# A graph kernel whose GpSimd gathers and scatters also wait for TensorE's place in the timetable, with a group's first gathers spread out

## The chip, the core and the metric

One core of a Trainium2 chip. The metric is device time in microseconds of one execution. The kernel before takes 2197.76 us, the median of three runs (2191.9 to 2199.88).

## What is computed

Two graph layers over 16 batches of 1024 nodes with 256 features, all in fp32. The first is an attention, the second weighs the edges of the adjacency matrix `adj` by a score of their two ends:

```
feats  = x @ W1.T;  f = feats @ w2 + b2
h      = softmax(leaky_relu(f[:,None] + f[None,:]) + adj) @ feats + bias2 + x
hidden = relu((h @ Wu)[u] + (h @ Wv)[v] + b1)             # for each pair u, v
S      = sigmoid(hidden @ w2' + b2')
z      = beta1*h + beta2*(((S*adj).T @ h) @ Wa + ba) + beta3*(((adj.T @ h) * h) @ Wm + bm)
```

`adj` is sparse, and S is needed only where it is not zero.

## The kernel before

The kernel computes S on the edges alone. At the start it makes a list of them: 135 slots of 128 edges, the same for all batches. The batches go in four groups of four, since one row that is gathered for an edge carries four batches.

For each batch TensorE does the attention: transposes (`turn`, `turn_e`), features, logits, products with the exponentials (`attend`, line 991, tile `pv`), then the ends of the edges (`end`, line 1028, tile `pp`), whose rows go to DRAM as `pu_d` and `pw_d`. VectorE takes `pv` out of PSUM in `keep_h` (lines 1002 and 1005, tiles `inv` and `xh`), and ScalarE copies the transposed result in `keep_hT` (line 1022, tile `hT`). The messages (line 1090, tile `pm`) and their products (line 1110, tile `pz`, taken up at line 1120) belong to the last term.

When the four batches of a group have their ends in DRAM, the group's 135 slots are scored (`scores`, line 1205), beside the attention of the next group. For a slot k:

- `fetch` (line 1140): GpSimd gathers, by an indirect DMA, 128 rows of `pw_d` into a `gv` buffer (line 1151, 1088 floats a row), and for the first slot of each of 21 lists also 128 rows of `pu_d` into `gu` (line 1144). There are 8 `gv` buffers, and slot k + 6 is fetched at the time of slot k (`AHEAD` is 6).
- `compare` (line 1180): VectorE, two instructions a slot, max and min of the two rows, in place.
- `sums` (lines 1191 and 1194): the sum over a row, on VectorE for some slots and on ScalarE for the others. This ends the use of the `gv` buffer.
- `gates`, and an addition (line 1221): the sigmoid of some 16 slots together, in a tile `lg`.
- `scatter` (line 1160): GpSimd writes 128 times four scores into `sa_d` in DRAM. Scatters that are ready wait in the list `late` and are emitted one or two a slot.

The scores of the first three groups fall into the time of the attention. After it, TensorE multiplies the scored edges by `h @ Wa` (`gather`, line 1284, tile `pzg`), which needs `sa_d` back in SBUF (`sat`, loaded by SP), turned by ScalarE (`part_sa`, line 1267) and multiplied by `adj` on VectorE (`weigh_sa`, line 1272). The fourth group is scored beside this work for the other groups, and its own product stands last.

The order of each engine's instructions comes from a timetable written by hand. `times.at(time, emit)` enters a piece of work at a moment; `times.matmuls(columns, emit)` enters TensorE's work at `times.now`, and moves that on by four cycles a column at 2.4 GHz. At the end all entries run in the order of their times, and each engine executes its instructions in that order, waiting only for data and free buffers. The times themselves play no part on the chip.

```
def at(self, time, emit):
    self.entries.append((time, len(self.entries), emit))

def matmuls(self, columns, emit):
    self.at(self.now, emit)
    self.now += columns * 4 / 2400
```

A group's slots share its stretch from `start` to `end` equally. In the function `first` of slot k stand the fetch of slot k + 6 and then the scatters of that moment; that of slot 0 is put 15 us earlier, and fetches slots 0 to 5 as well.

Of the kernel before, what the change touches and what calls it, by code (L numbers as in the profile page):

```python
# [14 lines left out]
P = 128  # L15
# [13 lines left out]
SLOTS = [(t, s) for t, width in enumerate(WIDTHS) for s in range(width)]  # L29
# [341 lines left out]
def edge_layers(  # L371
# [36 lines left out]
    nc = tc.nc  # L408
    B, N, D = x.shape
    C = N // P  # L410
    H = D // P
# [6 lines left out]
    p2 = ctx.enter_context(tc.tile_pool(name="p2", bufs=2, space=PSUM))  # L418
    ctx.enter_context(tc.manual_schedule())


    ident = const.tile([P, P], F32, name="ident")
    make_identity(nc, ident)
# [77 lines left out]
    for i in range(H):  # L501
        pt = p1.tile([P, BANK], F32, tag="p1", name="pt")
        for o in range(H):
            nc.tensor.transpose(pt[:, o * P : (o + 1) * P], w1_in[:, o, i * P : (i + 1) * P], ident)
        nc.vector.tensor_copy(w1T[:, i, :D], pt[:, :D])
        pw = p1.tile([P, BANK], F32, tag="p1", name="pw")
        for o in range(H):
            nc.tensor.matmul(
                pw[:, :1],
                lhsT=w1_in[:, o, i * P : (i + 1) * P],  # L510
                rhs=w2_col0[:, o, :],
                start=(o == 0),
                stop=(o == H - 1),
            )
        nc.vector.tensor_scalar(w1T[:, i, D : D + 1], pw[:, :1], 1.0 - SLOPE, None, ALU.mult)
# [36 lines left out]
    def rank_columns():  # L552
        nc.vector.tensor_scalar(up, w2_k, 0.0, None, ALU.is_ge)
        ps = p1.tile([P, BANK], F32, tag="p1", name="ps")
        nc.tensor.matmul(ps[:, 0:H], lhsT=upper, rhs=up, start=True, stop=True)
        nc.tensor.matmul(ps[:, H : 2 * H], lhsT=ones, rhs=up, start=True, stop=True)
        nc.vector.tensor_copy(signs, ps[:, : 2 * H])

    def place_columns():
# [31 lines left out]
    def turn_columns(i):  # L591
        pt = turned_w["pt", i] = p2.tile([P, 2 * BANK], F32, tag="p2", name="pt2")
        for k in range(H):
            for h in range(H):
                nc.tensor.transpose(
                    pt[:, (k * H + h) * P : (k * H + h + 1) * P],
                    uv_in[:, i, h, k * P : (k + 1) * P],
                    ident,
                )
# [7 lines left out]
    def sort_columns(i, h):  # L607
        pw = p1.tile([P, BANK], F32, tag="p1", name="pw")
        for k in range(H):
            nc.tensor.matmul(  # L610
                pw[:, :R],
                lhsT=turned_w[i][:, k, h * P : (h + 1) * P],
                rhs=to_place[:, i, k, :],
                start=(k == 0),
                stop=(k == H - 1),
            )
        nc.scalar.copy(wuv[:, i, h, :], pw[:, :R])

    def sort_bias():
        pw = p1.tile([P, BANK], F32, tag="p1", name="pw")  # L620
        for k in range(H):
            nc.tensor.matmul(
                pw[:, :R],
                lhsT=b1_rep[:, k, :],
                rhs=to_place[:, 0, k, :],
                start=(k == 0),
                stop=(k == H - 1),
            )
        nc.vector.tensor_copy(bu, pw[:, :R])
        nc.vector.memset(bu[:, HALF - 1 : HALF], -BIG)  # L630
# [22 lines left out]
    def edges():  # L653
# [76 lines left out]
        def placed():  # L730
# [20 lines left out]
            flat = pieces.rearrange("p k l -> p (k l)")  # L751
            yield
            pc = p1.tile([P, BANK], F32, tag="p1", name="pc")
            nc.tensor.matmul(pc[:, 0:K], lhsT=upper, rhs=flat, start=True, stop=True)
            nc.tensor.matmul(pc[:, K : 2 * K], lhsT=ones, rhs=flat, start=True, stop=True)
            yield
            total = keep.tile([P, K], F32, name="total0")
            nc.vector.tensor_copy(total, pc[:, K : 2 * K])
# [41 lines left out]
            nc.vector.tensor_reduce(over[:, 0:1], worst, AX.X, ALU.max)  # L800
            yield
            pl = p1.tile([P, BANK], F32, tag="p1", name="pl")
            nc.tensor.matmul(pl[:, :1], lhsT=ones, rhs=over[:, 0:1], start=True, stop=True)
            nc.vector.tensor_scalar(bad, pl[:, :1], 0.0, None, ALU.is_gt)
            yield

# [80 lines left out]
    def turn(b, h):  # L887

        pt = st["turn", b, h] = p2.tile([P, 2 * BANK], F32, tag="p2", name="pt2")
        for q in range(C):  # L890
            nc.tensor.transpose(
                pt[:, q * P : (q + 1) * P], held[b][:, q, h * P : (h + 1) * P], ident
            )

# [12 lines left out]
    def rows_of_f(b):  # L907

        pr = st["pr"] = p2.tile([P, 2 * BANK], F32, tag="p2", name="pr")
        for c in range(C):  # L910
            nc.tensor.transpose(
                pr[:, c * P : (c + 1) * P],
                st["f99"][:, c : c + 1].to_broadcast([P, P]),
                ident,
            )
# [5 lines left out]
    def features(b, c2):  # L921
        pf = st["pf", c2] = p2.tile([P, 2, BANK], F32, tag="p2", name="pf")
        for i in range(2):
            c = 2 * c2 + i
            for h in range(H):
                nc.tensor.matmul(  # L926
                    pf[:, i, : D + 1],
                    lhsT=st["xT"][:, h, c * P : (c + 1) * P],
                    rhs=w1T[:, h, :],
                    start=(h == 0),  # L930
                    stop=(h == H - 1),
                )
# [44 lines left out]
    def turn_e(b, c):  # L977
        e = st.pop(("e", b, c))
        pt = st["pt", b, c] = p2.tile([P, 2 * BANK], F32, tag="p2", name="pt2")
        for j in range(C):  # L980
            nc.tensor.transpose(pt[:, j * P : (j + 1) * P], e[:, j * P : (j + 1) * P], ident)  # L981

    def keep_eT(b, c):
        eT = st["eT", b, c] = two.tile([P, C, P], F32, name="eT")
# [2 lines left out]
    def attend(b, c):  # L987
        eT = st.pop(("eT", b, c))
        pv = st["pv", b, c] = p1.tile([P, BANK], F32, tag="p1", name="pv")
        for j in range(C):  # L990
            nc.tensor.matmul(  # L991
                pv[:, : D + 1],
                lhsT=eT[:, j, :],
                rhs=st["feats", b][:, j, :],
                start=(j == 0),
                stop=(j == C - 1),
            )
# [9 lines left out]
    def turn_h(b, i):  # L1007
        ph = st["ph", b, i] = p1.tile([P, H, 2 * P], F32, tag="p1", name="ph")
        for h in range(H):
            for k in range(2):  # L1010
                nc.tensor.transpose(
                    ph[:, h, k * P : (k + 1) * P],
                    held[b][:, 2 * i + k, h * P : (h + 1) * P],
                    ident,
                )
# [8 lines left out]
    def end(b, i, side, k):  # L1024

        pp = st["pp", side, k] = p1.tile([P, BANK], F32, tag="p1", name=f"pp{side}")
        for h in range(H):
            nc.tensor.matmul(  # L1028
                pp[:, :R],
                lhsT=st["hTi", b, i][:, h, k * P : (k + 1) * P],  # L1030
                rhs=wuv[:, side, h, :],
                start=(h == 0),
                stop=(h == H - 1),
            )
# [19 lines left out]
    def weighed(b, i):  # L1054
        pp = st["pea"] = p1.tile([P, 2, D], F32, tag="p1", name="pea")
        for k in range(2):
            for h in range(H):
                nc.tensor.matmul(  # L1058
                    pp[:, k, :],
                    lhsT=st["hTi", b, i][:, h, k * P : (k + 1) * P],  # L1060
                    rhs=wa[:, h, :],
                    start=(h == 0),
                    stop=(h == H - 1),
                )
# [21 lines left out]
    def message(b, half, h):  # L1086
        span = slice(half * BANK, (half + 1) * BANK)
        pm = st["pm", h] = p1.tile([P, BANK], F32, tag="p1", name="pm")
        for c in range(C):
            nc.tensor.matmul(  # L1090
                pm,
                lhsT=held[b][:, c, h * P : (h + 1) * P],
                rhs=adj_sb[:, c, span],
# [11 lines left out]
    def product(b, i):  # L1105
        pz = st["pz", i] = p1.tile([P, 2, D], F32, tag="p1", name="pz")
        for k in range(2):
            at = (2 * i + k) * P % BANK
            for h in range(H):
                nc.tensor.matmul(  # L1110
                    pz[:, k, :],
                    lhsT=st["mT"][:, h, at : at + P],
                    rhs=wm[:, h, :],
# [21 lines left out]
    AHEAD = 6  # L1135
# [4 lines left out]
    def fetch(g, k):  # L1140
        t, s = SLOTS[k]
        if s == 0:
# [5 lines left out]
                in_offset=bass.IndirectOffsetOnAxis(ap=key_u[:, t : t + 1], axis=0),  # L1148
            )
        gv = st["gv", k] = pools["gath"].tile([P, G * R], F32, name="gv", bufs=GV)  # L1150
        nc.gpsimd.indirect_dma_start(  # L1151
            out=gv,
            out_offset=None,
            in_=pw_d[g],
            in_offset=bass.IndirectOffsetOnAxis(ap=idx_v[:, t, s : s + 1], axis=0),
        )

    def scatter(g, lg, i, k):
        t, s = SLOTS[k]
# [7 lines left out]
        )  # L1167
        tc.declare_no_dep(dma.ins, group=f"sa{g}", reason="edges of their own")
        tc.add_to_no_dep_group(f"sa{g}", dma.ins)

    def by_batch(tile):
        return tile.rearrange("p (g r) -> p g r", r=R)
# [32 lines left out]
    def scores(g, start, end, on_vector):  # L1205

        for k in range(len(SLOTS)):
            time = start + k * (end - start) / len(SLOTS)

            def first(k=k):  # L1210
                for n in range(AHEAD) if k == 0 else ():
                    fetch(g, n)
                if k + AHEAD < len(SLOTS):
                    fetch(g, k + AHEAD)
                for _ in range(min(len(late), 2 if len(late) > PARTS[0] - 4 else 1)):
                    late.pop(0)()

            def last(k=k):
# [4 lines left out]
                )  # L1223
                late.extend(lambda i=i: scatter(g, lg, i, k0 + i) for i in range(k1 - k0))

            times.at(time - (15.0 if k == 0 else 0.0), first)
            times.at(time + 0.1, lambda k=k: compare(k, 0))
            times.at(time + 0.9, lambda k=k: compare(k, 1))
            k0, k1 = place_of(k)
# [46 lines left out]
    def gather(g, vc, part):  # L1276
# [4 lines left out]
        if part == C // 2 - 1:  # L1281
            order.sort(key=lambda cj: cj[1])
        for c, j in order:
            nc.tensor.matmul(  # L1284
                st["pzg", g, vc][:, j, :],
                lhsT=apart[:, c, j, :],
                rhs=st["ha", g, 2 * part + c][:, j * D : (j + 1) * D],
# [223 lines left out]
    def check():  # L1511
# [3 lines left out]
        nc.vector.tensor_reduce(ends_f[:, 1:2], f_least, AX.X, ALU.min)  # L1515
        pe = p1.tile([P, BANK], F32, tag="p1", name="pe")
        for i in range(2):
            nc.tensor.matmul(
                pe[0:1, i * P : (i + 1) * P],
                lhsT=ends_f[:, i : i + 1],  # L1520
                rhs=ident,
# [164 lines left out]
```

## Time and profile before

| | |
|---|---|
| Median of three runs | 2197.76 us (2191.9 to 2199.88) |
| Span of the profiled execution | 2373.8 us |
| TensorE matmul busy | 2185.9 us (92%) |
| VectorE, ScalarE busy | 1729.1, 1450.4 us |
| GpSimd busy | 1393.5 us, of it gathers of `gv` 599.7 and scatters 626.6 |
| Mean granted TensorE clock | 0.962 |
| DMA: gathers and scatters' queue, SP's queue | 46.4%, 31.3% of 16 engines' span |

The profile is of one execution that was recorded as it ran; its own time is the span, from the first instruction to the last, and nothing of the execution lies around it in the record. A row of a group of instructions reads: line, engine, operation, tile written and tiles read, shapes, how many; busy time and mean of one in ns; then how long the engine stood idle just before them, and what ended most of that. "issue" means that the engine waited for nothing that the profile shows, and "remote" or "another core or an unknown queue" that the record doesn't name the releaser. "POOL" is GpSimd, "DVE" VectorE, "ACT" ScalarE, "PEld" the loads of TensorE's weights.

### The profile page before, as it was taken

To read this page: it belongs to the slowest core of one execution; us is meant where nothing else is said; L and a number is where in the kernel's file an instruction comes from. 1 tells how busy PE (TensorE), PEld (TensorE's weight loads), DVE (VectorE), ACT (ScalarE), POOL (GpSimd) and SP (SyncE) were. 2 spreads that over 40 slices of the span, in tenths; PEclk is the share of its full clock that TensorE was granted. 3 is DMA by queue.
4 is the path that set the end of the run, shared out by engine and by line. 5 is a ranking of instruction groups with operands and counts; after the bars stand their busy time and mean duration, and the time that the engine had idled before them with its cause. 6 is when DMAs were issued, how large, how long until landed. Compare 5 with 4: busy or idle time off the path is not lost.

```text
span 2373.8 us, 30418 instructions
## 1 busy us (share of the span) xinstructions
PE 2185.9 (92%) x9478; PEld 1678.3 (71%) x9478; DVE 1729.1 (73%) x2660; ACT 1450.4 (61%) x3820; POOL 1393.5 (59%) x1277
## 2 busy tenths in 40 slices
PE   7999999798888989999899888988889999999998
PEld 6888877576666676766676666667557768778687
DVE  6599658687676777777777776777658879889454
ACT  5544567475656565657575555657347778778454
POOL 2223125677667767666777666667657767777400
PEclk9999999899899999999999998989999999999999
DMA  6789888677777777777787777778799999999664
GB/s 237 261 322 337 303 328 255 200 248 226 231 229 228 235 237 240 225 218 237 232 247 240 232 224 218 228 219 274 253 327 369 355 367 404 357 407 404 232 221 148
DMA packets 282491, 638.19 MB, mean 269 GB/s; under 512 B 43218, under 2 KB 142546, under 8 KB 281042
## 3 DMA queue, kind: packets, MB, share of 16 engines
q0 software_dynamic: 109312, 349.81, 46.4%
q1 hardware_dynamic: 154450, 268.93, 31.3%
q10 hardware_dynamic: 18560, 17.44, 2.2%
q8 instruction: 77, 1.26, 0.2%
q14 instruction: 92, 0.75, 0.1%
HBM read 476.42 MB, written 159.78 MB: 268 GB/s over the span
## 4 chain that ended last, share of the span: by engine, by line
PE 62%; DVE 16%; issue 6%; ACT 6%; another core or an unknown queue 5%; DMA 2%; POOL 1%; SPq 0%; POOLq 0%; ACTq 0%; DVEq 0%
PE pzg L1284 19%; PE pm L1090 12%; PE pv L991 11%; DVE gv L1180 7%; PE pp L1028 7%; PE pf L926 4%; PE pz L1110 3%; PE pea L1058 3%; DVE lg L1191 3%; PE pt L981 2%; ACT gv L1194 2%; DVE e L969 2%; ACT e L962 1%; DMA xh<-in_x_dram 1%
## 5 line engine op out<-in xcount | busy, mean ns | idle before, releaser
L1151 POOL DMA_INDIRECT gv<-pw_d,idx_v x540 | 599.7, 1111 | 382.3 <-ACT gv L1194 161.1
L1194 ACT ACTIVATE gv<-gv 128x272 f32<-128x272 f32 x1380 | 575.8, 420 | 362.8 <-DVE gv L1180 241.4
L1180 DVE TENSOR_TENSOR gv<-gv,gu 128x544 f32<-128x544 f32 x1080 | 735.2, 719 | 0.0
L1160 POOL DMA_INDIRECT sa_d<-lg,idx_s x540 | 626.6, 1160 | 181.2 <-issue 154.2
L991 PE MATMUL pv<-feats,eT 128*128 128x257 f32 x2048 | 480.7, 386 | 29.9 <-issue 21.1
L1090 PE MATMUL pm<-adj_sb,xh 128*128 128x512 f32 x1024 | 456.3, 598 | 7.5 <-issue 6.4
L1284 PE MATMUL pzg<-ha_g,apart 128*128 128x256 f32 x2048 | 450.4, 381 | 12.5 <-issue 12.5
L991 PEld LDWEIGHTS pv<-feats,eT 128*128 128x128 f32 x2048 | 385.7, 192 | 96.8 <-issue 33.9
L1284 PEld LDWEIGHTS pzg<-ha_g,apart 128*128 128x128 f32 x2048 | 391.2, 191 | 75.3 <-issue 22.0
L1090 PEld LDWEIGHTS pm<-adj_sb,xh 128*128 128x128 f32 x1024 | 194.5, 192 | 236.2 <-issue 232.4
L1028 PE MATMUL pp<-wuv,hT 128*128 128x272 f32 x1024 | 280.0, 420 | 67.4 <-ACT hT L1022 35.5
L1267 ACT COPY apart<-sat 128x1024 f32<-128x1024 f32 x128 | 255.5, 2005 | 70.0 <-PE pzg L1284 52.7
L1028 PEld LDWEIGHTS pp<-wuv,hT 128*128 128x128 f32 x1024 | 201.3, 203 | 124.4 <-ACT hT L1022 41.7
L1194 ACT ACTIVATION_READ_ACCUMULATOR gv<-gv 128x1 f32 x1380 | 261.2, 189 | 0.0
L1191 DVE TENSOR_REDUCE lg<-gv 128x4 f32<-128x1088 f32 x195 | 250.5, 1284 | 5.3
L1272 DVE TENSOR_TENSOR apart<-apart,adj_sb 128x1024 f32<-128x1024 f32 x128 | 156.7, 1224 | 99.2 <-ACT apart L1267 79.0
L969 DVE CUSTOM_DVE_ANT_0 e<-e,adj_sb 128x1024 f32<-128x1024 f32 x128 | 156.2, 1222 | 88.3 <-ACT e L962 45.9
L962 ACT ACTIVATE e<-frow,f 128x1024 f32<-128x1024 f32 x128 | 146.5, 1145 | 63.9 <-PE pt L981 23.7
L829 POOL DMA_INDIRECT table_d<-rec,at x52 | 56.3, 1083 | 198.1 <-DVE rec L824 176.8
L985 ACT COPY eT<-pt 128x1024 f32<-128x1024 f32 x128 | 127.8, 999 | 66.3 <-PE pp L1028 22.0
L975 ACT ACTIVATE e<-e,top 128x1024 f32<-128x1024 f32 x128 | 145.8, 1145 | 20.6 <-DVE top L969 20.1
L981 PE MATMUL pt<-ident,e 128*128 128x128 f32 x1024 | 136.5, 276 | 13.2 <-ACT e L975 8.1
(171 smaller groups left out, 1905.7 us busy)
## 6 DMA issues: line engine op xcount, KB each, us to landing
sa_d<-zero SPq DMA_DIRECT2D x128, 512.0 KB
sat<-sa_d SPq DMA_DIRECT2D x128, 512.0 KB
pu_d<-end SPq DMA_DIRECT2D x64, 272.0 KB
pw_d<-end SPq DMA_DIRECT2D x64, 272.0 KB
xh<-in_x_dram SPq DMA_DIRECT2D x16, 1024.0 KB
ha_d<-ea SPq DMA_DIRECT2D x64, 256.0 KB
zb_d<-zb SPq DMA_DIRECT2D x64, 256.0 KB
ha_g<-ha_d SPq DMA_DIRECT2D x32, 512.0 KB
```

The source lines that it names most:

```text
L969: nc.vector.tensor_tensor_reduce(e, e, adj_sb[:, c, :], -1.0, BIG, ALU.add, ALU.min, accum_out=top)
L981: nc.tensor.transpose(pt[:, j * P : (j + 1) * P], e[:, j * P : (j + 1) * P], ident)
L991: nc.tensor.matmul(pv[:, : D + 1], lhsT=eT[:, j, :], rhs=st["feats", b][:, j, :], start=(j == 0), stop=(j == C - 1),)
L1028: nc.tensor.matmul(pp[:, :R], lhsT=st["hTi", b, i][:, h, k * P : (k + 1) * P], rhs=wuv[:, side, h, :], start=(h == 0), stop=(h == H - 1),)
L1090: nc.tensor.matmul(pm, lhsT=held[b][:, c, h * P : (h + 1) * P], rhs=adj_sb[:, c, span], start=(c == 0), stop=(c == C - 1),)
L1151: nc.gpsimd.indirect_dma_start(out=gv, out_offset=None, in_=pw_d[g], in_offset=bass.IndirectOffsetOnAxis(ap=idx_v[:, t, s : s + 1], axis=0),)
L1160: dma = nc.gpsimd.indirect_dma_start(out=sa_d[g], out_offset=bass.IndirectOffsetOnAxis(ap=idx_s[:, t, s : s + 1], axis=0), in_=lg[:, i, :] ...
L1180: nc.vector.tensor_tensor(mv, mv, mu, op)
L1191: nc.vector.tensor_reduce(lg[:, i, :], one, AX.X, ALU.add)
L1194: nc.scalar.activation(one[:, j, :], one[:, j, :], AF.Copy, accum_out=lg[:, i, j : j + 1])
L1267: nc.scalar.copy(apart.rearrange("p c g v -> p c v g"), sat)
L1284: nc.tensor.matmul(st["pzg", g, vc][:, j, :], lhsT=apart[:, c, j, :], rhs=st["ha", g, 2 * part + c][:, j * D : (j + 1) * D], start=(part = ...
```

## The change

Each matmul and transpose is issued through a small function that remembers it, and each gather of `gv` and each scatter gets one more thing to wait for: the matmul or transpose that was emitted last before it. Gathers of `gu` get no wait of their own.

The second part is the place in the timetable. A group's first six gathers stand at 2.5 us from each other, 15 us to 2.5 us before the start, where they stood together; the seventh stands at the start. A scatter stands half a slot after the gather, and in every third slot one more may follow at 0.9 of the slot when more than 12 are left.

```
+    reached = {}
+
+    def matmul(*args, **kwargs):
+        reached["pe"] = nc.tensor.matmul(*args, **kwargs).ins
+
+    def transpose(*args, **kwargs):
+        reached["pe"] = nc.tensor.transpose(*args, **kwargs).ins
+
+    def after_tensor(dma):
+        tc.add_manual_dep(
+            dma.ins,
+            reached["pe"].name,
+            mybir.DependencyInfo(mybir.DependencyClass.Sync, mybir.DependencyReason.DATA),
+            reason="in step with TensorE",
+        )
...
-        nc.gpsimd.indirect_dma_start(
+        dma = nc.gpsimd.indirect_dma_start(
             out=gv,
             out_offset=None,
             in_=pw_d[g],
             in_offset=bass.IndirectOffsetOnAxis(ap=idx_v[:, t, s : s + 1], axis=0),
         )
+        after_tensor(dma)
...
         tc.add_to_no_dep_group(f"sa{g}", dma.ins)
+        after_tensor(dma)
...
-            def first(k=k):
-                for n in range(AHEAD) if k == 0 else ():
-                    fetch(g, n)
-                if k + AHEAD < len(SLOTS):
-                    fetch(g, k + AHEAD)
-                for _ in range(min(len(late), 2 if len(late) > PARTS[0] - 4 else 1)):
+            def half(k=k):
+                if late:
+                    late.pop(0)()
+
+            def extra(k=k):
+                if len(late) > PARTS[0] - 4:
                     late.pop(0)()
...
-            times.at(time - (15.0 if k == 0 else 0.0), first)
+            if k < AHEAD:
+                times.at(start - 2.5 * (AHEAD - k), lambda k=k: fetch(g, k))
+            if k + AHEAD < len(SLOTS):
+                times.at(time, lambda k=k: fetch(g, k + AHEAD))
+            times.at(time + (end - start) / len(SLOTS) / 2, half)
+            if k % 3 == 1:
+                times.at(time + (end - start) / len(SLOTS) * 0.9, extra)
```

In the rest of the diff, every `nc.tensor.matmul` and `nc.tensor.transpose` up to the edge products becomes `matmul` and `transpose`; in the profile of the changed kernel TensorE's work therefore stands under the two lines of those functions, 424 and 427.

More of the change, by code (lines that the diff above doesn't have):

```diff
@@ L503, in edge_layers @@
         for o in range(H):
-            nc.tensor.transpose(pt[:, o * P : (o + 1) * P], w1_in[:, o, i * P : (i + 1) * P], ident)
+            transpose(pt[:, o * P : (o + 1) * P], w1_in[:, o, i * P : (i + 1) * P], ident)
         nc.vector.tensor_copy(w1T[:, i, :D], pt[:, :D])
@@ L507, in edge_layers @@
         for o in range(H):
-            nc.tensor.matmul(
+            matmul(
                 pw[:, :1],
@@ L554, in rank_columns @@
         ps = p1.tile([P, BANK], F32, tag="p1", name="ps")
-        nc.tensor.matmul(ps[:, 0:H], lhsT=upper, rhs=up, start=True, stop=True)
-        nc.tensor.matmul(ps[:, H : 2 * H], lhsT=ones, rhs=up, start=True, stop=True)
+        matmul(ps[:, 0:H], lhsT=upper, rhs=up, start=True, stop=True)
+        matmul(ps[:, H : 2 * H], lhsT=ones, rhs=up, start=True, stop=True)
         nc.vector.tensor_copy(signs, ps[:, : 2 * H])
@@ L594, in turn_columns @@
             for h in range(H):
-                nc.tensor.transpose(
+                transpose(
                     pt[:, (k * H + h) * P : (k * H + h + 1) * P],
@@ L609, in sort_columns @@
         for k in range(H):
-            nc.tensor.matmul(
+            matmul(
                 pw[:, :R],
@@ L621, in sort_bias @@
         for k in range(H):
-            nc.tensor.matmul(
+            matmul(
                 pw[:, :R],
@@ L753, in placed @@
             pc = p1.tile([P, BANK], F32, tag="p1", name="pc")
-            nc.tensor.matmul(pc[:, 0:K], lhsT=upper, rhs=flat, start=True, stop=True)
-            nc.tensor.matmul(pc[:, K : 2 * K], lhsT=ones, rhs=flat, start=True, stop=True)
+            matmul(pc[:, 0:K], lhsT=upper, rhs=flat, start=True, stop=True)
+            matmul(pc[:, K : 2 * K], lhsT=ones, rhs=flat, start=True, stop=True)
             yield
@@ L802, in placed @@
             pl = p1.tile([P, BANK], F32, tag="p1", name="pl")
-            nc.tensor.matmul(pl[:, :1], lhsT=ones, rhs=over[:, 0:1], start=True, stop=True)
+            matmul(pl[:, :1], lhsT=ones, rhs=over[:, 0:1], start=True, stop=True)
             nc.vector.tensor_scalar(bad, pl[:, :1], 0.0, None, ALU.is_gt)
@@ L890, in turn @@
         for q in range(C):
-            nc.tensor.transpose(
+            transpose(
                 pt[:, q * P : (q + 1) * P], held[b][:, q, h * P : (h + 1) * P], ident
@@ L910, in rows_of_f @@
         for c in range(C):
-            nc.tensor.transpose(
+            transpose(
                 pr[:, c * P : (c + 1) * P],
@@ L925, in features @@
             for h in range(H):
-                nc.tensor.matmul(
+                matmul(
                     pf[:, i, : D + 1],
@@ L980, in turn_e @@
         for j in range(C):
-            nc.tensor.transpose(pt[:, j * P : (j + 1) * P], e[:, j * P : (j + 1) * P], ident)
+            transpose(pt[:, j * P : (j + 1) * P], e[:, j * P : (j + 1) * P], ident)
     def keep_eT(b, c):
@@ L990, in attend @@
         for j in range(C):
-            nc.tensor.matmul(
+            matmul(
                 pv[:, : D + 1],
@@ L1010, in turn_h @@
             for k in range(2):
-                nc.tensor.transpose(
+                transpose(
                     ph[:, h, k * P : (k + 1) * P],
@@ L1027, in end @@
         for h in range(H):
-            nc.tensor.matmul(
+            matmul(
                 pp[:, :R],
@@ L1057, in weighed @@
             for h in range(H):
-                nc.tensor.matmul(
+                matmul(
                     pp[:, k, :],
@@ L1089, in message @@
         for c in range(C):
-            nc.tensor.matmul(
+            matmul(
                 pm,
@@ L1109, in product @@
             for h in range(H):
-                nc.tensor.matmul(
+                matmul(
                     pz[:, k, :],
@@ L1283, in gather @@
         for c, j in order:
-            nc.tensor.matmul(
+            matmul(
                 st["pzg", g, vc][:, j, :],
@@ L1517, in check @@
         for i in range(2):
-            nc.tensor.matmul(
+            matmul(
                 pe[0:1, i * P : (i + 1) * P],
```

## Prediction

> **What bounds the kernel now.** I read the head of the page first, then the table by stage, the groups, GpSimd's own waits, and one stall in the timeline.
>
> ```profile
> span 2373.8 us, 30418 instructions
> ...
> PE 2185.9 (92%) x9478; PEld 1678.3 (71%) x9478; DVE 1729.1 (73%) x2660; ACT 1450.4 (61%) x3820; POOL 1393.5 (59%) x1277
> ```
>
> The profiled execution has a span of 2373.8 us, the runs a median of 2197.76: it is 176.0 us (8%) longer. All sums below are made in the profiled execution, and I say each time what of them can exist in the runs.
>
> The table by stage (us, then busy us and instructions of PE, PEld, DVE, ACT, POOL; clock; DMA share; GB/s) says where TensorE loses time:
>
> ```profile
> 320.00:1245.00 925.00, 839.37 (x3576) 620.92 (x3575) 686.91 (x1100) 573.70 (x1727) 628.72 (x561) 0.96 0.77 236
> 1245.00:1770.00 525.00, 452.39 (x1827) 324.88 (x1826) 363.27 (x583) 292.44 (x928) 348.08 (x321) 0.92 0.77 244
> 1770.00:2235.00 465.00, 460.67 (x1925) 361.33 (x1924) 386.59 (x467) 348.45 (x892) 343.53 (x280) 0.99 0.97 363
> 2235.00:2374.00 139.00, 131.73 (x586) 110.94 (x584) 65.07 (x57) 65.15 (x33) 0.00 (x0) 0.98 0.63 209
> ```
>
> Matmul busy time overstates, so I took the spacing of matmul starts within a group as the price of one record (109 ns a transpose, 217 at 256 or 257 columns, 429 at 512). At those prices all of TensorE's work is 2092 us. In 320 to 1770 us it starts 236 us later than they allow; after 1770 it loses some 6 us in 600. So TensorE is the bound, and what can be won lies in the 1450 us where the edge gathers of groups 0 to 2 run beside the attention.
>
> GpSimd's transfers, and the vector work that uses them:
>
> ```profile
> L1151 POOL DMA_INDIRECT gv<-pw_d,idx_v x540 | 599.7, 1111 | 382.3 <-ACT gv L1194 161.1
> ...
> L1180 DVE TENSOR_TENSOR gv<-gv,gu 128x544 f32<-128x544 f32 x1080 | 735.2, 719 | 0.0
> L1160 POOL DMA_INDIRECT sa_d<-lg,idx_s x540 | 626.6, 1160 | 181.2 <-issue 154.2
> ```
>
> The last column is what matters: the 1080 comparisons were never kept waiting (0.0), so no gather arrives late here. Taking the landings of each gather from the trace, the median one is issued 5 to 8 us before it lands and lands 14 us before its comparison; the tightest has 2.4 us left. GpSimd, in turn, mostly waits for a buffer:
>
> ```profile
> POOL gv L1151 <- ACT gv L1194: 161.1, 80, 9.7
> ...
> POOL gv L1151 <- DVE lg L1191: 41.7, 18, 6.0
> ```
>
> Eight gv buffers and a gather issued six slots ahead mean that it can lead by two slots at most.
>
> Half of TensorE's 236 us has a strange look. The timeline near 730 us (start, duration, what, idle before it and who ended it):
>
> ```profile
> 727.13 3.64 PE L991 MATMUL pv<-feats,eT 128*128 128x257 f32 x16
> ...
> 734.48 0.96 POOL L1151 DMA_INDIRECT gv<-pw_d,idx_v  x1 [0.31 <-issue]
> ...
> 739.56 1.01 POOL L1160 DMA_INDIRECT sa_d<-lg,idx_s  x1 [0.30 <-issue]
> 741.44 0.17 DVE L1002 RECIPROCAL inv<-pv 128x1 f32<-128x1 f32 x1 [11.32 <-remote]
> ```
>
> The matmuls that inv needs end at 730.77 by the record, yet inv starts at 741.44, just after GpSimd ran dry at 740.57. TensorE's semaphore itself moves at 741.42. There are 35 such stretches, 190 us long together; TensorE loses 119 us in or next to them, and 117 us elsewhere, mostly behind VectorE and ScalarE in their fixed order.
>
> **The change, part by part.** The order of instructions is the same on TensorE, VectorE, ScalarE and SP; only GpSimd's differs. So every direct cost is on GpSimd's queue, and reaches TensorE only through a late gather or a late last scatter.
>
> *The waits.* Built, 361 of the 540 gathers and 294 of the 540 scatters carry a wait on TensorE; the others come after one that covers them. A wait is for the last matmul emitted before it, so it ends with that whole group, up to 3.4 us after the timetable's moment. Behind a waiting transfer stand all later ones of GpSimd; who needs those are the comparisons and, at the end, the load of sat. I laid the new order and waits over the record of before, with TensorE, buffers, lg and each transfer's duration as they were: gathers start a median of 3.2, 2.4, 2.1 and 4.4 us later in groups 0 to 3, scatters about 5 us. Of the gathers as they were, 43, 32, 36 and 74% started before TensorE had reached their place. With 5.4 us to land, the median gather keeps 10 to 12 us; 3 of 540 come late, by 1.6 us at most. The price is 0 to 2 us here. If that cover were gone, it is what the slower rival below pays.
>
> Here the Trainium skill speaks against the change: "DMA: Bandwidth & Descriptors", Rules for kernel authors, says to issue a transfer early and to wait for its semaphore late. By that rule each group's delay is paid, some 12 us over the four. By the L1180 row, with 0.0 us before 1080 comparisons, the lead given up was not in use, and the sum is 0. I follow the row for the likeliest case.
>
> *The waiting instructions.* GpSimd gets 464 more of them (693 become 1157). The pause between two transfers is 304 to 305 ns whether none (385 pairs) or one (256 pairs) stands between: they pass under the transfer before. Price 0; uncovered, at 17 to 43 ns (least and median recorded), 8 to 20 us of GpSimd's time. TensorE raises its semaphore in 11 more matmuls: no price is visible for that.
>
> *Scatters at half a slot, extras every third slot.* The same 1080 transfers. Transfers beside a comparison take 1204 ns on average, beside a VectorE instruction that reads one SBUF tensor (L1191) 994, and comparisons themselves stay at 708 to 721 ns. If every scatter left the comparisons alone, GpSimd would save at most some 540 x 0.21 x 0.35 = 40 us, the 0.35 being the share of transfers that overlap one (413 of 1164); nobody waits for it. The other bound is nothing, as actual starts follow buffers and not the timetable. I take 0.
>
> *First gathers spread.* Seven of them stood in one block, 15 us before a group's start, ahead of four or five scatters of the old group. Group 1's ran from 781.1 to 790.6 us, then paused until 797.3 for buffers. Spread, they let those scatters pass; neither is awaited. Price 0; bounds -7 us a border on GpSimd alone, and +0.
>
> *The end.* The last 14 scatters are placed at one moment, which TensorE reaches at 2221.6; before, the first of them started at 2213.9. Fourteen at 1.29 us end at 2239.7 and not 2234.2: 5.5 us later. SP waits for the last before loading sat (issue at 2235.51), ScalarE's copy of it ran 2239.41 to 2241.43, and VectorE took it up at 2247.08: 5.65 us in hand. Price 0 to 1 us; with no cover, 5.5.
>
> Sum: 0 to 3 us, that is 2374 to 2377 us of the profiled kind and about 2199 in the runs.
>
> **Rivals.**
>
> *Faster: the late semaphores shrink.* In those stretches GpSimd goes on with up to eleven transfers, and TensorE's semaphore moves as they end. A gather that waits for that very semaphore would stop, and the stretch would end sooner. Against it in the runs: the profiled execution is 176 us longer than they are, which is the size of these stretches; of TensorE's 236 us only 236 - 176 = 60 can be left in a run. Half of that won gives 2168; all of it, 2138.
>
> *Slower: GpSimd has no lead to give in the runs.* Its need is (599.7 + 626.6 + 96.1) + 1164 x 0.305 = 1677 us. In the profile it has from 318.6 to 2234.2, 1916 us. If the runs save their 176 us there, it has 1740, and is busy 96% of it: then lead that is thrown away is not got back. It decides once a group's delay exceeds what its gathers have in hand. Each of the four groups then pays its median delay, 3.2 + 2.4 + 2.1 + 4.4 = 12.1, and the end its 5.5: 17.6 us, 2215. At the 95th percentile of the delays (7.0, 6.7, 8.3 and 7.7, with 5.5) it is 35 us, 2233. For it speaks the 96%, and that comparisons get tighter when TensorE runs faster; against it, that a GpSimd which is behind finds TensorE's place already reached, and the wait costs nothing.
>
> *It does not do what it says:* GpSimd is behind TensorE anyway, the waits never bind, and the time stays at 2198.
>
> **How the numbers follow.** Differences under 0.5% (11 us) are about what a measurement of this kernel cannot tell from none. No change, by cover (0.33) or by waits that don't bind (0.10): 0.43, at 2199. Slower, 2215, reaching 2233: 0.32, since the runs are tighter than the profile and nothing here wins time for certain. Faster, 2168: 0.25. The range leaves out a tenth at each end: from just under 2168 to 2233. The likeliest case by itself spans 2190 to 2207.
>
> **What would show it.** In the profile after: TensorE among those that GpSimd's gathers wait for, with tens of us; still about 0.0 us idle before the comparisons (right) or several us (the slower rival); the share of "another core or an unknown queue" in the chain near 5% (right) or halved with a span under 2330 us (the faster rival, at least under the profiler); the last scatter some 5 us nearer to the first copy of group 3's sat, and no gap of TensorE over 2 us there. I am wrong if comparisons wait, or if a run without the profiler has more of the late semaphores than 60 us allow.

## The result and the profile after

The changed kernel takes 2209.36 us (median of seven runs, 2206.62 to 2218.44), the kernel before 2199.3 beside it (2191.9 to 2204.15): a ratio of 1.0051, with an interval of 1.0031 to 1.0072. That is 6.8 to 15.8 us slower, at the edge of the 0.5% I had set, and 10 us above the 2199 I had forecast. One thing has to be known to read any number below: on the four chips of my experiments (called A to D) the same kernel before takes 2384 to 2414 us, and the change, where it ran among them (B), makes it faster; the recorded execution of before (span 2373.8 us) looks like those, while the changed kernel's record (span 2210.3, own time 2212.04) is of the quicker kind.

The head of the changed kernel's page and its groups for the comparisons, scatters and gathers:

```profile
span 2210.3 us, 30883 instructions
...
PE 2127.9 (96%) x9478; PEld 1653.8 (75%) x9478; DVE 1730.4 (78%) x2660; ACT 1450.3 (66%) x3820; POOL 1387.0 (63%) x1277
...
L1198 DVE TENSOR_TENSOR gv<-gv,gu 128x544 f32<-128x544 f32 x1080 | 738.5, 719 | 112.2 <-DMA gv<-pw_d,idx_v 110.5
...
L1177 POOL DMA_INDIRECT sa_d<-lg,idx_s x540 | 625.0, 1157 | 196.3 <-issue 126.2
L1167 POOL DMA_INDIRECT gv<-pw_d,idx_v x540 | 597.3, 1106 | 222.1 <-issue 102.9
```

The comparisons, which had waited 0.0 us in the record of before, now wait 112.2, of it 110.5 for a gather. The gathers' own row changes too: 382.3 us of idle time before them, the largest part for buffers, are now 222.1. In GpSimd's own waits (what waits, for what: us in total, times, longest):

```profile
POOL sa_d L1177 <- PE pm L424: 25.1, 12, 6.4
...
POOL gv L1167 <- PE pv L424: 13.3, 11, 4.3
POOL gv L1167 <- ACT gv L1212: 11.6, 32, 1.2
POOL gv L1167 <- PE pm L424: 11.3, 4, 3.9
```

All rows that name TensorE sum to 88.3 us in 110 waits. The wait for ScalarE's buffer, 161.1 us before, is down to 11.6: GpSimd no longer runs ahead until the buffers stop it. The median gather lands 1.6, 1.7, 1.3 and 7.4 us before its comparison in the four groups, where it had 14 in the record of before.

The stages of the changed kernel (us, then busy us and instructions of PE, PEld, DVE, ACT and POOL, the clock, DMA share, GB/s):

```profile
320.00:1245.00 925.00, 895.91 (x3983) 677.00 (x3982) 765.58 (x1225) 636.59 (x1926) 700.73 (x624) 0.99 0.84 262
1245.00:1770.00 525.00, 503.78 (x2114) 373.63 (x2113) 427.56 (x631) 351.94 (x1057) 395.67 (x356) 0.99 0.92 310
```

TensorE gets through 3983 instructions in 925 us against 3576 in the record of before, and the clock is 0.99 against 0.92 to 0.96. At my prices by start spacing, TensorE's starts are late by 106.5 us in the whole of this execution; in the record of before it was 270. Not one stretch in which VectorE, ScalarE or TensorE stands over 0.8 us for an unnamed releaser is left, of 35 with 190 us. By itself that looks like a great success of the change. It isn't: the kernel before took 2199.3 us beside it, so most of this difference is not the change's.

### The profile page after: what moved, and what is told of

The parts are those of the page before. It is cut to its first block, busy times and chain, and to the rows that moved or that the text cites. A ratio compares the mean times of both kernels' runs of the same rounds, so it can differ in the third digit from the quotient of the medians.

```text
span 2210.3 us, 30883 instructions
## 1 busy us (share of the span) xinstructions
PE 2127.9 (96%) x9478; PEld 1653.8 (75%) x9478; DVE 1730.4 (78%) x2660; ACT 1450.3 (66%) x3820; POOL 1387.0 (63%) x1277
## 5 line engine op out<-in xcount | busy, mean ns | idle before, releaser
L1198 DVE TENSOR_TENSOR gv<-gv,gu 128x544 f32<-128x544 f32 x1080 | 738.5, 719 | 112.2 <-DMA gv<-pw_d,idx_v 110.5
L1177 POOL DMA_INDIRECT sa_d<-lg,idx_s x540 | 625.0, 1157 | 196.3 <-issue 126.2
L1167 POOL DMA_INDIRECT gv<-pw_d,idx_v x540 | 597.3, 1106 | 222.1 <-issue 102.9
L424 PE MATMUL pv<-feats,eT 128*128 128x257 f32 x2048 | 470.4, 382 | 9.3 <-ACT eT L1001 6.9
L424 PE MATMUL pzg<-ha_g,apart 128*128 128x256 f32 x2048 | 452.3, 382 | 11.6 <-DVE apart L1296 11.6
L424 PE MATMUL pm<-adj_sb,xh 128*128 128x512 f32 x1024 | 448.4, 592 | 0.4 <-DVE end L1057 0.4
L424 PEld LDWEIGHTS pv<-feats,eT 128*128 128x128 f32 x2048 | 382.3, 191 | 69.4 <-ACT eT L1001 9.6
L424 PE MATMUL pp<-wuv,hT 128*128 128x272 f32 x1024 | 256.5, 396 | 20.5 <-DVE xh L1021 16.9
L1296 DVE TENSOR_TENSOR apart<-apart,adj_sb 128x1024 f32<-128x1024 f32 x128 | 156.6, 1224 | 121.1 <-ACT apart L1291 121.0
L424 PEld LDWEIGHTS pp<-wuv,hT 128*128 128x128 f32 x1024 | 190.1, 191 | 64.4 <-issue 16.7
L427 PEld LDWEIGHTS pt<-ident,e 128*128 128x128 f32 x1024 | 120.3, 142 | 26.5 <-issue 10.1
```

Source lines behind the costliest of these rows:

```text
L424: reached["pe"] = nc.tensor.matmul(*args, **kwargs).ins
L427: reached["pe"] = nc.tensor.transpose(*args, **kwargs).ins
L1167: dma = nc.gpsimd.indirect_dma_start(out=gv, out_offset=None, in_=pw_d[g], in_offset=bass.IndirectOffsetOnAxis(ap=idx_v[:, t, s : s + 1], ...
L1177: dma = nc.gpsimd.indirect_dma_start(out=sa_d[g], out_offset=bass.IndirectOffsetOnAxis(ap=idx_s[:, t, s : s + 1], axis=0), in_=lg[:, i, :] ...
L1198: nc.vector.tensor_tensor(mv, mv, mu, op)
L1296: nc.vector.tensor_tensor(apart, apart, a.unsqueeze(2).to_broadcast([P, 2, G, P]), ALU.mult)
```

## The experiments

Three theories stood against each other at the start. Theory G is the slower rival of the prediction: in the runs GpSimd has no lead left, so a wait that binds throws time away (G+S adds that waits also shorten late stretches where there are any). Rival C: the cover of 10 to 14 us is there, and only the end costs. Rival P: the new places cost it, and not the waits.

Twelve runs, on chips A to D (A for the first four, B for the next four, C for the next three, D for the last). On none of them did the kernel before take near 2199 us. The record numbers the chips of the experiments and not that of the result; that the result is of another chip is inferred from the times, and below it is called the quicker chip. "Late stretches" are those just described, merged over the engines; "TensorE loses" is the sum of its late starts over the prices, in the whole execution.

| run | chip | ratio, interval | late stretches, us | TensorE loses, us | comparisons idle, us |
|---|---|---|---|---|---|
| before | A | 1.0019 [0.9995, 1.0042] | 34, 201 | 266 | 0.4 |
| waits only | A | 0.9706 [0.9655, 0.9757] | 35, 182 | 218 | 7.2 |
| places only | A | 0.9997 [0.997, 1.0025] | 39, 211 | 286 | 0.9 |
| change, end free | A | 0.9621 [0.9569, 0.9673] | 35, 133 | 195 | 6.9 |
| change | B | 0.96 [0.9566, 0.9634] | 44, 140 | 199 | 9.8 |
| before | B | 0.9996 [0.9975, 1.0017] | 47, 276 | 304 | 0.0 |
| change, gathers wait | B | 0.9626 [0.9595, 0.9656] | 45, 164 | 207 | 5.0 |
| change, scatters wait | B | 0.9602 [0.9567, 0.9636] | 41, 161 | 211 | 2.3 |
| before, seven buffers | C | 0.9903 [0.9864, 0.9941] | 38, 219 | 248 | 7.3 |
| change, seven slots ahead | C | 0.9633 [0.9588, 0.9679] | 38, 143 | 197 | 0.2 |
| before | C | one run | 35, 197 | 283 | 0.0 |
| before, fewer scatters | D | 0.9568 [0.9519, 0.9618] | 34, 165 | 198 | 0.0 |

**The two parts apart (chip A).** First the kernel before, as it is:

> The kernel before once more, for an undisturbed profile of it (the recorded one was 176 us longer than its runs). Ratio 1.000. All theories: a span near 2200 us without the late TensorE semaphores. Theory G (GpSimd has no lead left in the runs, and waits that bind throw away time that it can't get back): gathers land with almost nothing in hand here too (median under 3 us), and comparisons wait for gathers by some 50 to 110 us in total. Rival C (the cover of 10 to 14 us is there in the runs as well, so the 11 us come from the end alone): comparisons wait 0 to 5 us, and the median gather has over 8 us in hand.

It took 2385.34 us. This overturns the first step of my sums: the execution whose profile is shown (2371.16 us for a span of 2369.5) is no longer than the 21 others beside it (2372.7 to 2401.74). (Each of these has a span and a clock on record too, so what a run with nothing recorded takes there isn't known.) The stretches are there as well, in the waits of VectorE and ScalarE for a releaser without a name:

```profile
DVE inv L1002 <- remote: 95.0, 13, 15.2
ACT hT L1022 <- remote: 50.1, 7, 14.0
```

At worst VectorE stood 15.2 us before an inv, after matmuls of 3.6 us. Where such a consumer was idle, the time from the recorded end of the matmul group to its start is 0.04 us in the median, but some 11 us at the 95th percentile and 23 at most; in the changed kernel's record on the quicker chip it is never over 0.1. This count needs no name of a releaser. The names are less sure: on all of A to D, and in the record of before, half or less of the completions of GpSimd's transfers are in the record (43 to 50%; in the changed kernel's record on the quicker chip 99.8%), so a wait "for a releaser without a name" can be one whose end is missing.

The waits without the new places:

```
         dma = nc.gpsimd.indirect_dma_start(      # the gather of gv, in fetch
...
+        after_tensor(dma)
...
         tc.add_to_no_dep_group(f"sa{g}", dma.ins) # the scatter
+        after_tensor(dma)
```

> The waits on TensorE alone, with the old places of gathers and scatters. Theory G: the waits are the cost, ratio to before 1.004 to 1.008 (2207 to 2216 us). Rival P (the new places cost it: gathers at a group's start have less lead): 1.000. Rival C: 1.002 to 1.003, the 5 us of the end.

```profile
span 2321.8 us, 30688 instructions
...
L1198 DVE TENSOR_TENSOR gv<-gv,gu 128x544 f32<-128x544 f32 x1080 | 735.5, 719 | 7.2 <-DMA gv<-pw_d,idx_v 4.6
```

0.9706: the waits make the kernel faster on this chip, by 3%, which none of the three theories had, and the comparisons wait 7.2 us in all. There the cover is real (the median gather still lands 8 to 11 us before its comparison in each group), and giving lead away costs next to nothing.

The new places without the waits, that is, the changed kernel less its two calls:

```
-        after_tensor(dma)
...
-        after_tensor(dma)
```

> The new places alone, without the waits. Theory G: ratio to before 0.998 to 1.001. Rival P: 1.004 to 1.006. Rival C: 1.000.

0.9997. The places alone do nothing, and the rival that charged them with the cost falls, as far as this kind of chip goes. And the whole change, but with the scatters that stand after the fourth group's last slot free of the wait:

```
-    def scatter(g, lg, i, k):
+    def scatter(g, lg, i, k, wait=True):
...
-        after_tensor(dma)
+        if wait:
+            after_tensor(dma)
...
         if g + 1 == NG:
-            times.at(ended, lambda: [late.pop(0)() for _ in range(len(late))])
+            times.at(ended, lambda: [late.pop(0)(False) for _ in range(len(late))])
```

> The changed kernel, in which only the scatters that are placed after the last slot of the fourth group don't wait for TensorE. Theory G: the end is a small part, ratio to before 1.003 to 1.005, 1 to 3 us less than the changed kernel. Rival C: the end is all of it, 1.000 to 1.001.

0.9621, about 1% better than the waits at the old places on the same chip (the runs don't overlap: 2282.43 to 2301.7 us against 2308.49 to 2323.46). Two things differ there, the places and the free end, and they weren't taken apart. TensorE's first product behind the last scatters, for which it waits 3.03 us in the changed kernel's record on the quicker chip, isn't waited for at all here, and not in the kernel before either.

**The change itself, and which of its waits does it (chip B).** The changed kernel and the kernel before, both unaltered, side by side:

> The changed kernel once more, beside the kernel before on the same chip. Two kinds of chip have been seen: one on which the kernel before takes 2199 us, one on which it takes 2384 us and TensorE's semaphores come late for 190 to 210 us of the profile. Theory G+S (the waits cost lead that GpSimd lacks, and shorten the late stretches where there are any): ratio 1.003 to 1.007 on the first kind, 0.96 to 0.97 on the second. Rival (the gain of the first four runs came from something else than the waits): 1.00 on the second kind too.

> The kernel before, for its profile on this chip. On a chip where it takes 2199 us: no late semaphores, comparisons wait for gathers (50 to 110 us, theory G) or not (0 to 5 us, rival C: there is cover). On one where it takes 2384 us: as in the first four runs, 190 to 210 us of late semaphores, comparisons wait 0 to 1 us.

The changed kernel is 4% faster here and 0.5% slower on the quicker chip. Its page and GpSimd's waits:

```profile
span 2302.1 us, 30883 instructions
...
L1198 DVE TENSOR_TENSOR gv<-gv,gu 128x544 f32<-128x544 f32 x1080 | 735.9, 719 | 9.8 <-DMA gv<-pw_d,idx_v 9.7
```

```profile
POOL sa_d L1177 <- PE pm L424: 30.8, 15, 6.4
POOL sa_d L1177 <- remote: 15.9, 15, 2.0
...
POOL gv L1167 <- PE pv L424: 13.1, 8, 4.3
POOL gv L1167 <- remote: 12.3, 9, 2.9
```

GpSimd waits much as on the quicker chip: the rows that name TensorE sum to 105.9 us in 83 waits, those without a name to 28.3 in 24. But the gathers land 8 to 10 us ahead of their comparisons (medians of the four groups), so comparisons hardly wait. Waits at the new places, on gathers alone or on scatters alone:

```
         tc.add_to_no_dep_group(f"sa{g}", dma.ins)
-        after_tensor(dma)
```

> The changed kernel with the wait on the gathers alone; scatters go as soon as their data and GpSimd's queue allow. Theory G+S: gathers are what fills the buffers and the DMA queue, so most of the effect stays: on a chip at 2199 us 1.002 to 1.006, on one at 2384 us 0.965 to 0.975. Rival (it is the scatters' 128 small writes that disturb TensorE): 1.000 on both.

```
             in_offset=bass.IndirectOffsetOnAxis(ap=idx_v[:, t, s : s + 1], axis=0),
         )
-        after_tensor(dma)
```

> The changed kernel with the wait on the scatters alone. A scatter that waits holds the gathers behind it too, GpSimd being one queue. Theory G+S: half to all of the effect: on a chip at 2199 us 1.001 to 1.005, on one at 2384 us 0.965 to 0.985. Rival (gathers alone matter, and holding the queue at every other place does nothing): 1.000 on both.

0.9626 and 0.9602: either kind alone gives all of it, a little more than was expected of either. That fits gathers and scatters standing in one queue, where a wait on one holds the other too. Tabled over the stretch from 320 to 1770 us, the kernel before on chip A, then the changed kernel on chip B:

```profile
320.00:1770.00 1450.00, 1299.37 (x5442) 952.05 (x5441) 1056.33 (x1689) 873.51 (x2663) 987.83 (x888) 0.95 0.77 240
```

```profile
320.00:1770.00 1450.00, 1343.17 (x5710) 992.49 (x5709) 1112.30 (x1757) 922.13 (x2795) 1020.07 (x923) 0.97 0.81 257
```

In the same time TensorE does 5710 instructions for 5442 (for 5336 in the kernel before on chip B itself). What goes is the loss in and next to the late stretches, 133 and 164 us in the kernel before on A and B, 60 us in the change; outside them TensorE loses about as much as ever (93 and 94 before, 101 in the change). The stretches get shorter, not fewer: 201 us in 34 (5.9 us each) and 276 in 47 (5.9) before, 140 in 44 (3.2) in the change, and 3.6 and 3.9 with one kind of wait. The waits at the old places shorten them less, to 5.2, and gain less.

**A cap, or the wait (chip C).** If it only matters that GpSimd gets less far ahead, a buffer less should do it too:

```
-GV = 8
+GV = 7
```

> The kernel before with seven buffers for gathered rows in place of eight, and no wait on TensorE. GpSimd can then run one slot less ahead, held back by a buffer and not by TensorE's counter. Cap theory: on a chip where the kernel before takes near 2390 us, the change gains because it holds GpSimd back at all, so a smaller cap should give part of the 4%: 0.97 to 0.99. Wait theory: it is the wait on TensorE itself, which stops GpSimd only while TensorE stands and so lets TensorE's counter through, and a buffer's wait on ScalarE doesn't do that: 1.00, within 0.005, and late stretches of 190 us or more as before. Theory of lost cover: the smaller lead lets comparisons wait for gathers, 1.00 to 1.02. On a chip where the kernel before takes near 2199 us no theory gives a gain: 1.00 to 1.01.

```profile
L1180 DVE TENSOR_TENSOR gv<-gv,gu 128x544 f32<-128x544 f32 x1080 | 735.5, 719 | 7.3 <-DMA gv<-pw_d,idx_v 7.0
```

1% faster, a quarter of the change's gain: at the end of what the cap theory had (0.97 to 0.99), and more than the wait theory had (1.00, within 0.005). Its late stretches are as long as ever (219 us in 38, 5.8 us each; TensorE loses 140 in and next to them, against 128 in the kernel before beside it), so the 1% comes from elsewhere, and where isn't shown. A smaller lead by itself doesn't shorten them. Then the changed kernel with an earlier place for its gathers, to give it lead back:

```
-    AHEAD = 6
+    AHEAD = 7
```

> The change with gathers seven slots ahead of their comparison in place of six (eight buffers as now), so that a gather's place in TensorE's timetable is one slot, about 3 us, earlier. If the changed kernel's gathers are late because their places leave too little lead, then on a chip where the kernel before takes near 2199 us the comparisons' idle time falls from 112 us to under 40 and the ratio from 1.005 to 1.000 or a little less. If GpSimd is simply full there (3.0 us of a slot's 3.0), the earlier place changes nothing: idle 100 or more, ratio 1.005. On a chip where the kernel before takes near 2390 us: 0.955 to 0.965 as with six if the gain comes from the scatters' waits, up to 0.98 if a looser hold on the gathers gives a part of it back.

```profile
L1198 DVE TENSOR_TENSOR gv<-gv,gu 128x544 f32<-128x544 f32 x1080 | 735.7, 720 | 0.2 <-issue 0.2
```

The comparisons' waiting goes, 9.8 to 0.2 us, and the time stays (0.9633): on these chips TensorE wasn't paying for it. Whether more lead helps on the quicker chip, the question it was made for, stays untested. And the kernel before once more, for a record that could have come from a quicker chip, and did not:

> The kernel before once more, for a profile on this chip. If the chip is one where it takes near 2199 us: no late stretches at all (none over 0.8 us put down to another core or an unknown queue), a span near 2197, and either comparisons that wait for gathers by well under the change's 110 us, which would put the change's cost on its waits, or by as much, which would leave only the end (last scatter 5 us earlier than in the change, counted from the last pooling product). If it is one of the others: a span of 2370 to 2410, over 190 us of late stretches, comparisons' idle under 1 us.

**Fewer transfers, no wait (chip D).** The kernel before without one scatter in four in the first three groups:

```
-                late.extend(lambda i=i: scatter(g, lg, i, k0 + i) for i in range(k1 - k0))
+                late.extend(
+                    lambda i=i: scatter(g, lg, i, k0 + i)
+                    for i in range(k1 - k0)
+                    if g + 1 == NG or (k0 + i) % 4
+                )
```

> The kernel before, which leaves out one slot's scatter in four in the first three groups (102 of 540), so that their outputs lack those scores. No wait is added. On a chip where the kernel before takes near 2390 us, the theory that late stretches come with the density of GpSimd's transfers lets them shrink from about 200 us by a tenth to a third, and the ratio falls to 0.96 to 0.99; a theory by which only waiting on TensorE helps leaves 1.00, since GpSimd runs as far ahead as its buffers let it either way; a theory by which GpSimd's freed time just lets it run ahead and do its gathers in a denser row gives 1.00 or a little more. On a chip where it takes near 2199 us, a GpSimd that has no time left there (3.0 us of work in a slot of 3.0) would make the kernel faster by what its transfers cost TensorE, 0.98 to 0.995, with no wait of the comparisons left; if TensorE alone sets the time, it is 1.00.

```profile
span 2302.1 us, 30215 instructions
...
PE 52%; DVE 23%; ACT 8%; issue 7%; another core or an unknown queue 4%; DMA 3%; POOL 1%; SPq 0%; POOLq 0%; ACTq 0%; DVEq 0%
...
L1180 DVE TENSOR_TENSOR gv<-gv,gu 128x544 f32<-128x544 f32 x1080 | 734.8, 719 | 0.0
L1160 POOL DMA_INDIRECT sa_d<-lg,idx_s x438 | 505.1, 1153 | 159.7 <-issue 124.6
```

0.9568, as much as the change gives (and just past the 0.96 to 0.99 expected), with no wait on TensorE anywhere; TensorE's loss in and next to late stretches is 82 us. So a wait for TensorE is not the only cure; a GpSimd with 102 transfers less to do is another, with 34 stretches of 4.9 us.

What the two have in common the traces don't show. If waits broke up GpSimd's rows of transfers (with pauses under 0.6 us), the rows would be shorter in the change; the longest is 59 us there, 44 in this kernel, and 51 to 86 in the four records of before, so the change stands among those. A dense row isn't enough to make a semaphore late either: the changed kernel on the quicker chip has one of 1082 us and not a single late one. In the kernel before, 18 of 34 stretches (A) and 25 of 47 (B) end within 3 us after GpSimd ran dry, where chance would give 16 to 18%. Either the stop lets the semaphore through, or both follow from a machine that stands still and frees no buffer; these runs can't tell the one from the other.

## Why the prediction was right or wrong

**The first reading was wrong.** "The profiled execution has a span of 2373.8 us, the runs a median of 2197.76: it is 176.0 us (8%) longer", and I took the difference for one between a profiled execution and runs. On A to D the profiled execution and the others beside it agree, at 2384 to 2414 us, and the records have the late stretches; so the record of before and the runs of 2197.76 us are of two kinds, most likely of two chips. With it falls the figure "only 236 - 176 = 60 can be left in a run": in the record after, on the quicker chip, there are no late stretches at all, and in the kernel before on chip A TensorE loses 226 us in those 1450.

**The waits: price 0 to 2 us by cover.** On chips A and B, where waits were tried with six slots ahead, right: comparisons idle by 2.3 to 9.8 us. On the quicker chip wrong: 110.5 us. The step that failed is "with 5.4 us to land, the median gather keeps 10 to 12 us": that was worked out on a record where TensorE loses 236 us and GpSimd can use them to get ahead. On A and B the median gather kept 8 to 11; on the quicker chip 1.6, 1.7, 1.3 and 7.4 in the four groups. Here the rule of the Trainium skill that I had set aside for the row of before ("DMA: Bandwidth & Descriptors", Rules for kernel authors: issue early, wait late) stood on the right side: it spoke for a loss, and the change measured one, 11.2 us by the ratio. (That I had 12 us for the groups by it confirms nothing, since the 11.2 aren't taken apart.) On A and B the row was right and the rule was not: there issuing later gained 3 to 4%.

**The slower rival fits best, and is not shown.** It said that GpSimd needs 1677 us and has 1740. In the record after its transfers take 597.3 + 625.0 + 93.5 us and its pauses 1164 x 0.305 = 355, together 1671, between 322.6 and 2076.8 us, which is 1754: 95% busy. The 83 us that are left are about the 88 us of waits for TensorE. The size was off, 17.6 us against 11.2 (6.8 to 15.8), because a comparison's wait isn't TensorE's. In 320 to 1770 us TensorE has 57.3 us of losses over 0.3 us; 24.8 of them come within 8 us after a comparison that waited, and since a third of all moments do (33%), some 19 would by chance; so TensorE's losses hardly point to the comparisons. The largest row of TensorE's waits in that stretch is of VectorE's xh, which stands in its fixed order behind comparisons:

```profile
PE pp L424 <- DVE xh L1021: 16.7, 12, 3.6
```

How much of this the kernel before has on such a chip isn't known, as there is no record of it there. An estimate from the record after: with GpSimd's transfers laid one behind the other in their order, with their durations, buffers and scores as recorded but no wait for TensorE, the median gather would land 6.1, 1.7, 1.8 and 11.9 us before its comparison in the four groups (1.6, 1.6, 1.2 and 7.9 by the same working with the waits, against 1.6, 1.7, 1.3 and 7.4 measured). So in groups 1 and 2 GpSimd has next to no lead even without the waits, and part of the 112 us would stand in the kernel before as well. Of the 11 us some 3 are the end's, by the rows below; that the rest comes from the comparisons' waits is argued from the record after, and not shown by taking a part away on such a chip.

**The end: price 0 to 1 us, 5.5 without cover.** The timeline of the changed kernel there (start, duration, what, idle before it and who ended it):

```profile
2075.88 0.97 POOL L1177 DMA_INDIRECT sa_d<-lg,idx_s  x1 [0.31 <-issue]
...
2078.83 1.40 SPq L1278 DMA_DIRECT2D sat<-sa_d  x3
...
2082.58 1.94 ACT L1291 COPY apart<-sat 128x1024 f32<-128x1024 f32 x1 [16.05 <-DMA sat<-sa_d]
...
2084.56 1.23 DVE L1296 TENSOR_TENSOR apart<-apart,adj_sb 128x1024 f32<-128x1024 f32 x1 [7.36 <-ACT apart L1291]
2085.84 10.15 PE L424 MATMUL pzg<-ha_g,apart 128*128 128x256 f32 x32 [3.03 <-DVE apart L1296]
```

ScalarE waits 16.05 us for sat, VectorE 7.36 for the copy, TensorE 3.03 for VectorE's product. I had read 5.65 us in hand and put the price at no more than 1. It is 3.0: TensorE waits 0 us at this product in all four records of the kernel before, and without waits on the last scatters (end free; gathers wait), but 3.4 us in the change on B, 3.4 with waits on scatters alone, 3.6 with seven slots ahead and 1.1 with the waits at the old places. The term was undersized, and the cap of 5.5 held.

**What held.** The places alone: 0.9997 on A, where I had 0. (With the waits they, or the free end, are worth about 1% there, which I had not foreseen.) The waiting instructions: the pause between two transfers is 304 to 305 ns in the record after too, with one in between or none. No single stall of TensorE after 1770 us exceeds 3.2 there. One bound was too low, though the price of 0 doesn't rest on it: I counted 413 of 1164 transfers as beside a comparison; any overlap at all have 772, 365 of them scatters, which take 1224 ns against 1027 without one, so the bound is some 70 us of GpSimd's time and not 40.

**The faster rival** was right about what a wait does to the late stretches, and right in its sign on A and B (and, with seven slots ahead, on C). On B TensorE's losses fall from 304 us to 199 and the median by 96; on A, with the end free, from 266 to 195 and by 87. It was wrong, on the quicker chip, about there being anything to win. The sign I had set for it, a span under 2330 us with fewer unnamed waits, came true all the same (2210.3 us, no late stretch) beside a kernel that was 0.5% slower: that sign could not tell the change from another chip.

So the time came out within some 10 us of the forecast by luck, and not for its reason. By my own signs I was wrong: comparisons wait, and a gap of TensorE at the end is over 2 us. The cover that was to make the waits free is not in the record after, and what went with that, 11 us, was small.

## What to carry to other kernels

Before a profile is read as the kernel's, compare its span with the runs: if they differ by 8%, find out whether it was another chip, since slack measured on the slower one (14 us of lead before the change, 8 to 11 with the waits) may not exist on the other (1.3 to 1.7 us with the waits in three of the four groups). A queue that is 95% busy has little lead to give, but a late gather is only paid where the engine that sets the end stands behind it: 112 us of waiting comparisons went with 11 us of time, some 3 of which are the end's. And a gain that is the cure for one chip's trouble (4% here) should be measured on a chip without it before it is kept.

## What the runs showed of the hardware

The same program took 2199.3 us where the result was taken and 2383.67, 2406.73, 2388.88 and 2414.05 (medians) on chips A to D. Nearly all of the late stretches lie where gathers and scatters run beside the attention: from about 415 us on, TensorE's semaphores reach idle consumers up to 23 us after the recorded end of their matmuls. In the four records of the kernel before, stretches that begin before 1770 us sum to 181 to 239 us, and later ones, with the fourth group's transfers still running, to 4 to 36.

The granted clock falls along with it (0.92 to 0.96 in those stages, 0.99 without), and the traces show that it follows. Between 320 and 1770 us it drops to half 20 times in the kernel before on A, 23 on B, 16 in the change on B and 5 in its record on the quicker chip. Every drop comes after 3.4 us in which TensorE was busy for at most 0.52, 0.41, 0.50 and 0.42 of the time, where the averages are 0.90, 0.88, 0.93 and 0.97. In a drop matmuls start twice as far apart (428 ns for 217), which costs TensorE 35, 44, 25 and 7 us. So some 19 of the 105 us of losses that the change saves TensorE on B are the clock's, in the wake of shorter stops.

What holds the semaphore back on those chips stays open. That the same records lack half of the completions of GpSimd's transfers is a second difference from the quicker one; whether the two have one cause was not tried.
